# Four attention layers on one Trainium2 core: written orders for late fetches, additions and norms, and a quarter of a running sum moved to VectorE

## Chip, core and metric

The kernel runs on one core of a Trainium2 chip. The metric is the device time of one execution in microseconds; "before" is the median of three executions. The profile is one more execution, recorded by the hardware profiler. The engines are named as the profile names them: PE (TensorE, matmuls; PEld its weight loads), DVE (VectorE), ACT (ScalarE), POOL (GpSimd), SP (SyncE, which here only issues transfers).

## What is computed

Sixteen sequences of 56 tokens with 256 features pass through four layers. In each layer they attend to a memory of their own, 1500 rows of 128 features. Everything is float32. Cut to what matters, the reference is:

```python
def reference(x, ctx, mask, ...):                  # x 16x56x256, ctx 16x1500x128
    # L0: gated cross attention
    m = ctx @ W_mem
    c = softmax(x @ m.T / sqrt(D)) @ m
    x = rmsnorm(x + sigmoid(concat(x, c) @ W_gate + b) * c)
    # L1 (and L3, the same with other weights): masked cross attention, 16 heads, then a feed-forward part
    q = layernorm(x) @ Wq * scale;  k, v = split(ctx @ Wkv)
    x = x + tanh(attn_gate) * (softmax(where(mask, q @ k.T, lowest)) @ v) @ Wo
    x = x + tanh(ff_gate) * gelu(layernorm(x) @ W1) @ W2
    # L2: two experts (v, l) chosen by token, causal self attention, cross attention, MLP
    qkv = where(vm, rms(x) @ v_qkv, rms(x) @ l_qkv)
    x = x + where(vm, ctx_self @ v_dense, ctx_self @ l_dense)
    ck, cv = split(ctx @ ckv_w)                    # 16 heads of 8
    x = x + softmax(rms(x) @ cq_w @ ck.T) @ cv @ cdense_w
    mi = rms(x)
    x = x + where(vm, silu(mi @ v_gate) * (mi @ v_up) @ v_down,
                      silu(mi @ l_gate) * (mi @ l_up) @ l_down)
    # L3: as L1
    return x
```

The memory mask hides at most the last 375 of the 1500 rows.

## The kernel before

**Groups and items.** The 16 sequences ("batches") are four groups of four; a group has 224 tokens, kept as two tiles of 112 rows by 256. The pairs (layer, group) are sixteen items, k = 0 to 15. While an item's attention runs, side work is woven into it: the part behind the item before (`post`), and the part ahead of the next (`pre`). Side work is written as generators; `pace` and `step` draw pieces from them between the pieces of the attention, by shares that are written out by hand (`SHARES` for layer 2). The order in which the program emits the instructions is only a proposal: a scheduler puts them in the final order of each engine from the dependencies and its own estimates. Two copies of the program exist for two kinds of masks; the profiled execution runs the copy that masks the last 384 columns only.

**Layer 2's cross attention (`att2`).** Each batch has 12 chunks of 125 memory rows, taken as six pairs, one pair a step. All heads of a batch are 896 columns (4 row groups of PE, 224 columns each). One step of batch b, pair j, is:

- `weights_pair`: four banks of PSUM get the shifts (L1411, a matmul with ones) and then the scores (L1420, 32 matmuls in all); ScalarE takes the exponentials, one of 125x448 for each bank (L1425; 448 columns are both chunks of 224); then the weights are added into the running sum `all`, 125x896, in halves of 448 columns (L1437): POOL for batches 0 to 14, VectorE for batch 15. In the first pair of a batch there are two such additions, in each of the others four.
- `largest`: scores of the *next* batch for its maxima, four matmuls into four banks (L1374), and four reductions on VectorE (L1379). The maxima become the shifts (`shifts`, L1387 to L1400).
- `sums_chunk` (L1450): PE multiplies the weights of the pair before with the values.
- keys and values of coming batches (L1345, L1357), and pieces of side work.

Seven banks of PSUM rotate among all of these in the order of allocation; so the banks of the next L1411 come free only when the reductions L1379 of earlier banks are done. At the end of a batch `own_sums` (L1476 to L1484) takes the sums of `all` over its 125 rows with a matmul, and at the end of a group `close_group` (L1494) adds the result to the stream and starts the norm that is sorted by expert (`begin_norm`, sort: POOL scatters the rows to `sorted_rows`).

**Late side work in layer 2 (`late`, `beside`).** The part of L1 behind the attention (`post13`) runs for groups 2 and 3 only during layer 2; it has a `pause` between its two halves, and the second half begins with a layer norm: statistics on VectorE (L327, L328, L332), the root on POOL (L319), the normalization (L336, one operation for each of two tiles) on VectorE, and the turn by PE (L310 in `to_T`). Then `post2` takes the MLP of two groups at once: rows come from `sorted_rows` (`rows_of`), are turned (`to_T`, L310), multiplied (L1610), gated (L1617), multiplied back (L1629) and written to `made_rows`. `fetch` brings a group's rows back with two indirect transfers, issued by POOL (L1647); `take` adds them to the stream on VectorE (L1655) and begins the norm of L3. Groups 0 and 1 are taken while layer 2 still runs its group 3, groups 2 and 3 beside L3.

**L3's (and L1's) attention** takes rows of scores: L596 on PE, L599 on VectorE (mask and minimum), L603 on ScalarE (exponential), L633 the transposes, L614 the sums.

Of the kernel before, what the change touches and what calls it, by code (L numbers as in the profile page):

```python
# [15 lines left out]
AF = mybir.ActivationFunctionType  # L16
ALU = mybir.AluOpType
# [45 lines left out]
def tile_kernel(ctx: ExitStack, tc: tile.TileContext, a, layers=4, groups=NG):  # L63
# [239 lines left out]

    def to_T(xn, some=range(NT)):

        p = mm()
        w = len(some) * TP
        for c in range(2):
            for n, i in enumerate(some):
                nc.tensor.transpose(  # L310
                    p[:, c * w + n * TP : c * w + (n + 1) * TP],
                    xn[:, i, c * 128 : (c + 1) * 128],
                    ident[:TP, :TP],
                )
        return p[:, : 2 * w].rearrange("p (c t) -> p c t", c=2)

    def inverse_root(y, v):

        nc.gpsimd.tensor_tensor(y, v, half_less[:TP, : y.shape[-1]], ALU.pow)  # L319

    def begin_layernorm(g, gi, some=range(NT), engine=nc.gpsimd):
# [12 lines left out]
        xn = xpool.tile([TP, NT, D], F32, tag="xn", bufs=3, name="xn")  # L334
        for i in some:
            engine.tensor_scalar(  # L336
                xn[:, i, :], x[:, i, :], mv[:, 2 * i : 2 * i + 1], rstd[:, i : i + 1],
                ALU.subtract, ALU.mult,
            )
        begun[g, gi] = xn  # L340

    def layernorm_T(gi, g, b, some=range(NT)):
        if (g, gi) not in begun:
            begin_layernorm(g, gi, some, nc.vector)
            yield
            yield
        p = to_T(begun.pop((g, gi)), some)
        xT = xpool.tile([128, 2, T], F32, tag="xT", bufs=5, name="xT")[:, :, : len(some) * TP]
        gc, bc = VEC[g], VEC[b]
        for c in range(2):  # L350
            nc.vector.tensor_scalar(
                xT[:, c, :], p[:, c, :], vecs[:, gc + c : gc + c + 1],
                vecs[:, bc + c : bc + c + 1], ALU.mult, ALU.add,
            )
        return xT
# [224 lines left out]
    def rows(u):  # L580
# [12 lines left out]
        for i in range(RB):  # L593
            if u:
                sc = mm()
                nc.tensor.matmul(  # L596
                    sc[:, :LW], u["q"][:, i * 128 : (i + 1) * 128], u["kt"], start=True, stop=True
                )
                nc.vector.tensor_tensor_reduce(  # L599
                    u["p"][:, i], sc[:, :LW], u["mask"], 1.0, -LOWEST,  # L600
                    ALU.add, ALU.min, mn[:, i : i + 1],
                )
                nc.scalar.activation(  # L603
# [442 lines left out]
    def post13(name, gi, state, some=range(NT), pause=None):  # L1046
# [34 lines left out]
        w1, w2 = state["w1"], state["w2"]  # L1081
        xT = yield from layernorm_T(gi, name + "_ln_ff_g", name + "_ln_ff_b", some)
        yield
# [239 lines left out]
    PAIRS = NC // 2  # L1323
    SHARES = (2.1, 1.8), (2.1, 1.4), (2.1, 1.5), (1.8, 1.8)

# [39 lines left out]
    def largest(b, n):  # L1365
# [12 lines left out]
        for g in range(4):  # L1378
            nc.vector.tensor_reduce(  # L1379
                made["mx"][:, half * 4 + g, s : s + 1], banks[g][: 2 * N, :SW], AX.X, ALU.max  # L1380
            )

# [20 lines left out]
    def weights_pair(b, j):  # L1403
# [25 lines left out]
        if j == 0:  # L1429
            made["all"] = big.tile([128, 2, H, N], F32, tag="ot", name="all")[:CP, 0].rearrange(  # L1430
                "p h n -> p (h n)"
            )
        for c in range(0 if j else 1, 2):
            for lo in range(0, R, R // 2):
                cols = slice(lo, lo + R // 2)
                engine = nc.gpsimd if b + 1 < B else nc.vector
                engine.tensor_tensor(  # L1437
                    made["all"][:, cols], made["all"][:, cols] if j else p[:, 0, cols],
                    p[:, c, cols], ALU.add,
                )  # L1440

# [79 lines left out]
    def att2(gi, state, then, ends):  # L1521

        for k in range(G):
            b = gi * G + k
            for j in range(PAIRS):
# [15 lines left out]
                if ahead < B and not full:  # L1541
                    largest(ahead, n_ahead)
                if j + 2 == PAIRS and b + 1 < B:
                    shifts(b + 1)
# [24 lines left out]
    def post2(pair):  # L1569
# [21 lines left out]
        rows = rows_of(0)  # L1591
        yield
        yield
        for n, e in enumerate("vbl"):
            p = to_T(rows)
            xT = xpool.tile([128, 2, T], F32, tag="xT", bufs=5, name="xT")
# [46 lines left out]
    def fetch(gi):  # L1643

        y = tmp("back")[:TP]
        for i in range(NT):
            nc.gpsimd.indirect_dma_start(  # L1647
                y[:, i * D : (i + 1) * D], None, made_rows[gi // 2],
                bass.IndirectOffsetOnAxis(place_of(gi, i), 0),
            )  # L1650
        return y

    def take(gi, y):
        xf = xs[gi].rearrange("p i d -> p (i d)")
        nc.vector.tensor_add(xf, xf, y)  # L1655
        if gi < 3:
            begin_layernorm("L3_ln_q_g", gi)

    def program():
        line.update(turn=None, sum=None, side=iter(()), rate=1, closed=0, pair=None, due=0.0, share=0.0, k=0, behind=0, end=False, stage=0, beside=0)  # L1660
        for kept in (memory_w, halves_of, queries, heads_w, cross, held, begun):
# [23 lines left out]
        def beside(k):  # L1685
# [27 lines left out]
            if k == 3 * groups + 1:  # L1713
# [3 lines left out]
                yield  # L1717
                y = fetch(2)
                yield
                yield  # L1720
# [45 lines left out]
        def late():  # L1766
# [20 lines left out]
            y = fetch(0)  # L1787
            yield
            yield
            take(0, y)  # L1790
            line["stage"] += 1
            y = fetch(1)
            yield
            yield
            take(1, y)
# [211 lines left out]
```

## Time and profile before

| what | value |
|---|---|
| median of 3 runs | 1467.6 us (1466.56 to 1472.07) |
| the profiled execution's own time | 1461.5 us |
| its span | 1459.5 us |
| mean clock granted to PE | 0.981 of full speed |
| PE busy | 1370.9 us |
| 440–620 us: PE, DVE, ACT, POOL busy of 180 | 170.4, 97.3, 82.2, 108.8 |
| 620–780: of 160 | 152.3, 93.2, 78.5, 111.1 |
| 780–862: of 82 | 78.6, 54.4, 37.8, 56.1 |
| 862–1037: of 175 | 175.0, 90.5, 84.5, 140.8 |
| 1037–1060: of 23, clock 0.78 | 15.1, 9.0, 6.7, 17.7 |

The span goes from the first to the last instruction; some 2 us of the execution's time lie round it. Layer 2's cross attention runs from about 440 to 1085 us: group 0 to 620, group 1 to 780, group 2 to 862, and group 3 and the ends behind it. "Busy" sums the instructions of an engine in a stretch; the clock is what the throttle granted PE, where 1.0 is full speed. A wait is written "engine, tile, line <- the engine, tile and line that ended it", with its total, its count and the longest, in microseconds.

### The profile page before, as it was taken

The numbers are of one execution on the slowest core, as the hardware profiler recorded it, in microseconds if no ns is written. First come the engines' busy times: TensorE is split into PE (matmuls) and PEld (weight loads), VectorE is DVE, ScalarE is ACT, GpSimd is POOL, SyncE is SP. The second block draws the span as 40 slices with busy tenths as digits, with TensorE's granted clock in tenths as the row PEclk, the third lists the DMA queues.
The fourth block names the chain that finished last, engine by engine and source line by source line (L and its number), as shares of the span: only waits on it lengthen the run. The fifth ranks groups of instructions, "written<-read, shape, count | busy, mean of one in ns | idle before, by whom it ended". The sixth has DMA issues, their size and how long they took to land. (4 is left out here: it accounts for less than half of the span.)

```text
span 1459.5 us, 32402 instructions
## 1 busy us (share of the span) xinstructions
PE 1370.9 (94%) x13638; PEld 944.3 (65%) x13638; DVE 784.0 (54%) x1796; ACT 745.2 (51%) x1697; POOL 525.2 (36%) x567
## 2 busy tenths in 40 slices
PE   7989999999899989999999999999798999999997
PEld 4767777776655546555555556656466776777776
DVE  5344764557474753566546754554464345554641
ACT  2335767675533545444544544444365464756661
POOL 0021010100204656766577768787733111100000
PEclk9999999999999999999999999999899999999998
DMA  8943232331312011200110022131123343333320
GB/s 286 361 167 129 65 129 102 116 115 51 114 62 80 16 66 52 79 29 23 65 65 23 29 70 68 50 102 55 45 79 104 114 155 107 109 104 133 96 97 10
DMA packets 38808, 135.78 MB, mean 93 GB/s; under 512 B 8605, under 2 KB 18493, under 8 KB 34557
## 3 DMA queue, kind: packets, MB, share of 16 engines
q1 hardware_dynamic: 33901, 119.03, 23.8%
q0 software_dynamic: 2592, 10.85, 2.2%
q10 hardware_dynamic: 2160, 3.74, 0.7%
q8 instruction: 109, 1.79, 0.5%
q14 instruction: 46, 0.38, 0.1%
HBM read 129.01 MB, written 4.59 MB: 92 GB/s over the span
## 5 line engine op out<-in xcount | busy, mean ns | idle before, releaser
L1437 POOL TENSOR_TENSOR all<-all,pw 125x448 f32<-125x448 f32 x300 | 340.9, 1148 | 137.0 <-ACT pw L1425 126.7
L1379 DVE TENSOR_REDUCE mx<-sc 112x1 f32<-112x500 f32 x384 | 233.7, 669 | 127.7 <-PE sc L1374 127.5
L1425 ACT ACTIVATE pw<-sc 125x448 f32<-125x448 f32 x384 | 177.7, 550 | 116.2 <-PE sc L1420 113.2
L603 ACT ACTIVATE p<-p,few 128x384 f32<-128x384 f32 x224 | 136.9, 612 | 101.4 <-DVE few L599 100.7
L596 PE MATMUL sc<-ktl,qa 128*128 128x384 f32 x448 | 179.8, 510 | 0.0
L599 DVE CUSTOM_DVE_ANT_0 p<-sc,mkl 128x384 f32<-128x384 f32 x224 | 121.7, 551 | 93.7 <-PE sc L596 88.2
L614 PE MATMUL sc<-p,kvl 32*128 32x224 f32 x2160 | 153.7, 355 | 5.9 <-DVE qa L912 3.7
L614 PEld LDWEIGHTS sc<-p,kvl 32*128 32x128 f32 x2160 | 138.1, 186 | 22.3 <-issue 10.5
L614 PE MATMUL o<-p,kvl 32*128 32x224 f32 x720 | 146.8, 355 | 0.7 <-issue 0.6
L143 POOL TENSOR_SCALAR mkl<-m32l 128x384 bf16<-128x384 uint8 x32 | 16.3, 510 | 345.9 <-DVE few L599 300.2
L614 PEld LDWEIGHTS o<-p,kvl 32*128 32x128 f32 x720 | 131.5, 186 | 1.5 <-issue 1.5
L1374 PE MATMUL sc<-ck,qs 32*112 32x500 f32 x768 | 124.6, 625 | 4.1 <-DVE mx L1379 1.8
L302 ACT ACTIVATE p<-p,few 128x384 f32<-128x384 f32 x224 | 120.7, 609 | 7.5 <-DVE few L590 7.5
L633 DVE STREAM_TRANSPOSE p<-p 128x768 f32<-128x768 f32 (+1 forms) x96 | 103.0, 1095 | 23.0 <-ACT p L302 22.7
L596 PEld LDWEIGHTS sc<-ktl,qa 128*128 128x128 f32 x448 | 79.6, 193 | 37.5 <-issue 10.1
L1420 PE MATMUL sc<-qs,ck 32*125 32x224 f32 x1536 | 102.1, 362 | 0.0
L302 ACT ACTIVATE ot<-sc 128x224 f32<-128x224 f32 x64 | 32.0, 608 | 125.4 <-PE o L614 77.6
L1450 PE MATMUL o<-pw,vc 125*32 125x224 f32 x1536 | 95.8, 368 | 0.0
L1450 PEld LDWEIGHTS o<-pw,vc 125*32 125x32 f32 x1536 | 40.9, 111 | 70.1 <-issue 57.8
L319 POOL TENSOR_TENSOR stat<-stat,half_less 112x2 f32<-112x2 f32 (+1 forms) x33 | 23.1, 700 | 174.9 <-DVE stat L332 136.7
L1420 PEld LDWEIGHTS sc<-qs,ck 32*125 32x125 f32 x1536 | 79.6, 188 | 1.3
L1411 PE MATMUL sc<-shift,ones_r 2*125 2x448 f32 x384 | 61.5, 473 | 17.9 <-DVE mx L1379 15.4
(283 smaller groups left out, 2333.4 us busy)
## 6 DMA issues: line engine op xcount, KB each, us to landing
kvl<-in_ctx_last SPq DMA_DIRECT2D x30, 768.0 KB, 4.3
kt<-in_ctxT SPq DMA_DIRECT2D x23, 750.0 KB, 4.7
w<-in_L_W SPq DMA_DIRECT2D x16, 1024.0 KB, 4.8
w<-in_L_Wq SPq DMA_DIRECT2D x8, 1024.0 KB, 5.2
w<-in_L_Wo SPq DMA_DIRECT2D x8, 1024.0 KB, 4.8
ktl<-in_ctxT SPq DMA_DIRECT2D x32, 192.0 KB, 2.6
w<-in_L_v_qkv SPq DMA_DIRECT2D x4, 768.0 KB, 5.5
w<-in_L_l_qkv SPq DMA_DIRECT2D x4, 768.0 KB, 4.3
```

The costliest lines, as they stand in the source:

```text
L302: nc.scalar.activation(out, in_, AF.Copy, scale=scale)
L596: nc.tensor.matmul(sc[:, :LW], u["q"][:, i * 128 : (i + 1) * 128], u["kt"], start=True, stop=True)
L599: nc.vector.tensor_tensor_reduce(u["p"][:, i], sc[:, :LW], u["mask"], 1.0, -LOWEST, ALU.add, ALU.min, mn[:, i : i + 1],)
L603: nc.scalar.activation(u["p"][:, i], u["p"][:, i], AF.Exp, bias=mn[:, i : i + 1], scale=-1.0, accum_out=den[:, i : i + 1],)
L614: product = nc.tensor.matmul(o[g][:, : RB * BW], y["kv"][part, j, :], y["p"][part, :, j * BW : (j + 1) * BW], start=j == 0, stop=j == LB - ...
L633: nc.vector.transpose(blocks, blocks)
L1374: nc.tensor.matmul(banks[g][: 2 * N, :SW], made["q"][part, rows], made["k"][part, cols], start=True, stop=True,)
L1379: nc.vector.tensor_reduce(made["mx"][:, half * 4 + g, s : s + 1], banks[g][: 2 * N, :SW], AX.X, ALU.max)
L1420: nc.tensor.matmul(banks[g][:CP, c * QH : (c + 1) * QH], made["k"][part, at : at + CP], made["q"][part], start=False, stop=c == 1, skip_gr ...
L1425: nc.scalar.activation(p[:, :, g * QH : (g + 1) * QH], banks[g][:CP, : 2 * QH].rearrange("p (c n) -> p c n", c=2), AF.Exp,)
L1437: engine.tensor_tensor(made["all"][:, cols], made["all"][:, cols] if j else p[:, 0, cols], p[:, c, cols], ALU.add,)
L1450: nc.tensor.matmul(made["o"][part, :QH], made["v"][:, n, part], p[:, r * QH : (r + 1) * QH], start=n == 0, stop=n + 1 == NC, skip_group_ch ...
```

## The change

It has six parts. (1) A helper, `behind`, adds an ordering without a semaphore between two instructions: the first is put behind the second in the order that the scheduler makes. (2) The rows of pair 1 in `post2`: one more yield ahead of the first turn, and its transposes stand behind the last L596 that was emitted by then. (3) `begin_layernorm` gets a form for ScalarE: VectorE negates the mean (one small operation), and ScalarE subtracts it and multiplies with the root, two operations for each tile in place of VectorE's one. The late `post13` (groups 2 and 3) uses it. (4) `fetch` of groups 0 and 1 stands behind the last addition of weights on POOL, and `take`'s addition behind the last reduction of maxima (L1379) or of rows (L599). Four yields, not two, lie between fetch and take of groups 0 and 1, three, not two, for group 2. (5) The shares of groups 2 and 3 in layer 2 go from (2.1, 1.5) and (1.8, 1.8) to (2.1, 1.7) and (1.9, 1.9). (6) For batches 0 to 14 POOL adds the first three quarters of the weights' columns, in two operations of 336 columns where it had two of 448 for each chunk. VectorE adds the last 224 columns, which the fourth exponential makes; these additions are emitted at the end of the step's core, after the reductions of maxima. Batch 15 stays with VectorE in halves of 448.

```diff
--- before.py
+++ after.py
@@ -301,22 +301,34 @@
     def scalar_copy(out, in_, scale=1.0):
         nc.scalar.activation(out, in_, AF.Copy, scale=scale)
 
-    def to_T(xn, some=range(NT)):
+    def to_T(xn, some=range(NT), name=None):
 
         p = mm()
         w = len(some) * TP
         for c in range(2):
             for n, i in enumerate(some):
-                nc.tensor.transpose(
+                turned = nc.tensor.transpose(
                     p[:, c * w + n * TP : c * w + (n + 1) * TP],
                     xn[:, i, c * 128 : (c + 1) * 128],
                     ident[:TP, :TP],
                 )
+                behind(turned, name, "rows come late")
         return p[:, : 2 * w].rearrange("p (c t) -> p c t", c=2)
 
     def inverse_root(y, v):
 
         nc.gpsimd.tensor_tensor(y, v, half_less[:TP, : y.shape[-1]], ALU.pow)
+
+    def behind(made, name, reason):
+
+        if name:
+            tc.add_manual_dep(
+                made.ins, name,
+                mybir.DependencyInfo(
+                    mybir.DependencyClass.NoSync, mybir.DependencyReason.DATA
+                ),
+                reason=reason,
+            )
 
     def begin_layernorm(g, gi, some=range(NT), engine=nc.gpsimd):
 
@@ -332,16 +344,25 @@
         nc.vector.tensor_scalar(rstd[:, those], var, 1e-5, None, ALU.add)
         inverse_root(rstd[:, those], rstd[:, those])
         xn = xpool.tile([TP, NT, D], F32, tag="xn", bufs=3, name="xn")
-        for i in some:
+        if engine is nc.scalar:
+            less = stat(NT)[:TP]
+            mean = mv.rearrange("p (i s) -> p i s", s=2)[:, :, 0]
+            nc.vector.tensor_scalar(less, mean, -1.0, None, ALU.mult)
+            for i in some:
+                nc.scalar.activation(
+                    xn[:, i, :], x[:, i, :], AF.Identity, bias=less[:, i : i + 1]
+                )
+                scalar_copy(xn[:, i, :], xn[:, i, :], rstd[:, i : i + 1])
+        for i in () if engine is nc.scalar else some:
             engine.tensor_scalar(
                 xn[:, i, :], x[:, i, :], mv[:, 2 * i : 2 * i + 1], rstd[:, i : i + 1],
                 ALU.subtract, ALU.mult,
             )
         begun[g, gi] = xn
 
-    def layernorm_T(gi, g, b, some=range(NT)):
+    def layernorm_T(gi, g, b, some=range(NT), engine=None):
         if (g, gi) not in begun:
-            begin_layernorm(g, gi, some, nc.vector)
+            begin_layernorm(g, gi, some, engine or nc.vector)
             yield
             yield
         p = to_T(begun.pop((g, gi)), some)
@@ -593,13 +614,13 @@
         for i in range(RB):
             if u:
                 sc = mm()
-                nc.tensor.matmul(
+                line["scored"] = nc.tensor.matmul(
                     sc[:, :LW], u["q"][:, i * 128 : (i + 1) * 128], u["kt"], start=True, stop=True
-                )
-                nc.vector.tensor_tensor_reduce(
+                ).ins.name
+                line["drained"] = nc.vector.tensor_tensor_reduce(
                     u["p"][:, i], sc[:, :LW], u["mask"], 1.0, -LOWEST,
                     ALU.add, ALU.min, mn[:, i : i + 1],
-                )
+                ).ins.name
                 nc.scalar.activation(
                     u["p"][:, i], u["p"][:, i], AF.Exp, bias=mn[:, i : i + 1], scale=-1.0,
                     accum_out=den[:, i : i + 1],
@@ -1079,7 +1100,9 @@
         if "w2" not in state:
             (state["w2"],) = load_w((a[name + "_W2"], 8, D))
         w1, w2 = state["w1"], state["w2"]
-        xT = yield from layernorm_T(gi, name + "_ln_ff_g", name + "_ln_ff_b", some)
+        xT = yield from layernorm_T(
+            gi, name + "_ln_ff_g", name + "_ln_ff_b", some, nc.scalar if pause else None
+        )
         yield
         hT = big.tile([128, 8, T], F32, tag="hT", bufs=2, name="hT")[:, :, :w]
         per = 2 * T // w
@@ -1321,7 +1344,7 @@
 
     QH = 4 * N
     PAIRS = NC // 2
-    SHARES = (2.1, 1.8), (2.1, 1.4), (2.1, 1.5), (1.8, 1.8)
+    SHARES = (2.1, 1.8), (2.1, 1.4), (2.1, 1.7), (1.9, 1.9)
 
     def spread_queries(b):
 
@@ -1376,9 +1399,9 @@
                 start=True, stop=True,
             )
         for g in range(4):
-            nc.vector.tensor_reduce(
+            line["drained"] = nc.vector.tensor_reduce(
                 made["mx"][:, half * 4 + g, s : s + 1], banks[g][: 2 * N, :SW], AX.X, ALU.max
-            )
+            ).ins.name
 
     def shifts(b):
 
@@ -1430,14 +1453,21 @@
             made["all"] = big.tile([128, 2, H, N], F32, tag="ot", name="all")[:CP, 0].rearrange(
                 "p h n -> p (h n)"
             )
+        few_columns = 3 * R // 8 if b + 1 < B else R // 2
+        for lo in (0, few_columns):
+            add_weights(b, j, slice(lo, lo + few_columns), nc.gpsimd if b + 1 < B else nc.vector)
+
+    def add_weights(b, j, cols, engine):
+
+        made = cross[b]
+        p = made["p", j]
         for c in range(0 if j else 1, 2):
-            for lo in range(0, R, R // 2):
-                cols = slice(lo, lo + R // 2)
-                engine = nc.gpsimd if b + 1 < B else nc.vector
-                engine.tensor_tensor(
-                    made["all"][:, cols], made["all"][:, cols] if j else p[:, 0, cols],
-                    p[:, c, cols], ALU.add,
-                )
+            added = engine.tensor_tensor(
+                made["all"][:, cols], made["all"][:, cols] if j else p[:, 0, cols],
+                p[:, c, cols], ALU.add,
+            )
+            if engine is nc.gpsimd:
+                line["added"] = added.ins.name
 
     def sums_chunk(b, n):
 
@@ -1540,6 +1570,8 @@
                     sums_chunk(last, n + 1)
                 if ahead < B and not full:
                     largest(ahead, n_ahead)
+                if b + 1 < B:
+                    add_weights(b, j, slice(3 * R // 4, R), nc.vector)
                 if j + 2 == PAIRS and b + 1 < B:
                     shifts(b + 1)
                 if j == 1 and b:
@@ -1589,10 +1621,10 @@
         wc = VEC["L2_ln_post_attn_w"]
         wg, wu = (weights("v", w, 2, I2) for w in ("gate", "up"))
         rows = rows_of(0)
-        yield
-        yield
+        for _ in range(3 if pair else 2):
+            yield
         for n, e in enumerate("vbl"):
-            p = to_T(rows)
+            p = to_T(rows, name=line["scored"] if pair and not n else None)
             xT = xpool.tile([128, 2, T], F32, tag="xT", bufs=5, name="xT")
             for c in range(2):
                 nc.vector.tensor_scalar(
@@ -1644,20 +1676,22 @@
 
         y = tmp("back")[:TP]
         for i in range(NT):
-            nc.gpsimd.indirect_dma_start(
+            fetched = nc.gpsimd.indirect_dma_start(
                 y[:, i * D : (i + 1) * D], None, made_rows[gi // 2],
                 bass.IndirectOffsetOnAxis(place_of(gi, i), 0),
             )
+            if gi < 2:
+                behind(fetched, line["added"], "weights are added first")
         return y
 
     def take(gi, y):
         xf = xs[gi].rearrange("p i d -> p (i d)")
-        nc.vector.tensor_add(xf, xf, y)
+        behind(nc.vector.tensor_add(xf, xf, y), line["drained"], "banks go first")
         if gi < 3:
             begin_layernorm("L3_ln_q_g", gi)
 
     def program():
-        line.update(turn=None, sum=None, side=iter(()), rate=1, closed=0, pair=None, due=0.0, share=0.0, k=0, behind=0, end=False, stage=0, beside=0)
+        line.update(turn=None, sum=None, side=iter(()), rate=1, closed=0, pair=None, due=0.0, share=0.0, k=0, behind=0, end=False, stage=0, beside=0, added=None, drained=None, scored=None)
         for kept in (memory_w, halves_of, queries, heads_w, cross, held, begun):
             kept.clear()
         load_first()
@@ -1716,6 +1750,7 @@
                 yield
                 yield
                 y = fetch(2)
+                yield
                 yield
                 yield
                 take(2, y)
@@ -1785,13 +1820,13 @@
             yield
             yield
             y = fetch(0)
-            yield
-            yield
+            for _ in range(4):
+                yield
             take(0, y)
             line["stage"] += 1
             y = fetch(1)
-            yield
-            yield
+            for _ in range(4):
+                yield
             take(1, y)
             line["stage"] += 1
             while line["closed"] < 3 * groups:
```

## The prediction, made before the changed kernel ran

> **What bounds the kernel now.** I read the page's busy shares first, then the groups, the waits, and the timeline round each long wait. TensorE (PE) is busy 94% of the span; VectorE (DVE) 54%.
>
> ```profile
> PE 1370.9 (94%) x13638; PEld 944.3 (65%) x13638; DVE 784.0 (54%) x1796; ACT 745.2 (51%) x1697; POOL 525.2 (36%) x567
> ...
> L1437 POOL TENSOR_TENSOR all<-all,pw 125x448 f32<-125x448 f32 x300 | 340.9, 1148 | 137.0 <-ACT pw L1425 126.7
> L1379 DVE TENSOR_REDUCE mx<-sc 112x1 f32<-112x500 f32 x384 | 233.7, 669 | 127.7 <-PE sc L1374 127.5
> ```
>
> So 88.6 us of the 1459.5 are open to an edit that only orders work. The waits of PE name the pieces that this change aims at:
>
> ```profile
> PE sc L1411 <- DVE mx L1379: 15.4, 6, 7.9
> ...
> PE sc L310 <- DVE xn L336: 5.7, 2, 3.2
> ...
> PE sc L310 <- DMA rows<-sorted: 5.3, 2, 3.9
> ```
>
> Each line gives total, count and longest. The longest maxima wait is seen whole in the timeline: VectorE sits 5.86 us in take(0)'s addition, waiting for a fetch, while finished score banks lie undrained behind it.
>
> ```profile
> 1043.46 0.69 DVE L1655 TENSOR_TENSOR x<-x,back 112x512 f32<-112x512 f32 x1 [5.86 <-DMA back<-made,place]
> ...
> 1047.89 2.43 DVE L1379 TENSOR_REDUCE mx<-sc 112x1 f32<-112x500 f32 x4
> ...
> 1048.62 0.73 PE L1411 MATMUL sc<-shift,ones_r 2*125 2x448 f32 x1 [7.88 <-DVE mx L1379]
> ```
>
> Then the clock is low: 1045.0 to 1055.2 is granted half speed, and 16 scores take 2.22 us where they took 0.93 at 943.5. PE idles until 1048.6 anyway, so 6.6 us of half clock lose 3.3. The same pattern, shorter, stands at 530.58 (2.72 us, then 6.8 us at half clock) and 703.15 (2.74 us, then 3.4):
>
> ```profile
> 530.25 2.41 DVE L336 TENSOR_SCALAR xn<-x,stat 112x256 f32<-112x256 f32 x2 [3.14 <-POOL stat L319]
> ...
> 532.58 1.25 DVE L1379 TENSOR_REDUCE mx<-sc 112x1 f32<-112x500 f32 x2
> ```
>
> VectorE waits 3.14 us for POOL's root (late post13's norm), with maxima behind it.
>
> **The change, part by part.** *Fetch and take(0).* The addition moves behind the last maxima, (14,3). All 11.2 us (7.88 + 3.3) would go, but in the built order L3's turns (L310 of group 0) now stand directly after L1394, ahead of L1411 of step (14,5). They need, after the maxima: the addition 0.69, L327/L328/L332 1.9, POOL's root 0.72, two POOL L336 of 1.22: 5.8 us; PE has 2.5 us of work queued ahead of them. New stall 3.3, with 1.7 of half clock likely: gain 6.2, say **6**; bounds 0 (the new wait as long as the old) and 11. The four fetch instructions (0.93 each) move past POOL's additions and are split in two; POOL is idle 20% there (140.8 busy of 175 us), which covers them; without it they would put 1.9 us per pair on the additions.
>
> *Late norms.* For groups 2 and 3 DVE's two L336 (0.62 each) become four ScalarE operations per group, plus one DVE negation of 0.17. Nothing of VectorE waits for POOL's root there any more. ScalarE waits instead; behind it are the Exps, but ScalarE is busy 82 of 180 us in 440–620, and four operations at L302's 0.61 make 2.4 per group. The stalls with their half clock are 2.72 + 3.3 and 2.74 + 1.7 = 10.5. An Exp held behind that ScalarE wait, up to 3.14, gives part back: **7**, bounds 3 and 10.
>
> [...]
>
> *Rows' turns of pair 1.* One more L596 pair (0.81) goes ahead of the transposes, into the 3.92 us wait for rows<-sorted: 0.8 for certain, 2.5 if 3.4 us of half clock behind it goes too (1.7): **1.5** (0.7 to 2.5).
>
> *take(2), fetch(2) and L3's norms.* One yield more and an addition behind L599: gaps of 1.4 and up to 3.3 of half clock may go, but the norm begins some 6 us later against PE's order, with 2 more L596 (0.8) as cover: 0 (-3 to +4). L3's ff norm at 1238.7 gets L901 ahead of it against 3.18 us: +1 (-1 to +2.5). Shares only repace side work, seen in the order above: nothing extra. Sum of gains 15.5, some **15** (7 to 25).
>
> *A quarter of the columns.* POOL's 330 additions shrink from 448 to 336 columns, 1.133 to 0.85 us, 93 us of POOL. Nobody waits for that: the view of L1437 shows 0.9 for L1476 and 0.7 for L1425. VectorE gets 165 additions of 125x224, two in a step (one in a pair's first). In the built order they stand *ahead of* the maxima in nearly every step from the second on, and they wait for the fourth Exp. Behind them are four maxima, behind those the banks of the next L1411. Their price:
>
> ```profile
> L1437 POOL TENSOR_TENSOR all<-all,pw x300: 1118/1133/1522, 457.3 to 1066.5; 125x448 f32<-125x448 f32 x150
> L1437 DVE TENSOR_TENSOR all<-all,pw x20: 617/624/626, 1068.7 to 1085.1; 125x448 f32<-125x448 f32 x20
> L1437 DVE TENSOR_TENSOR all<-pw x2: 1555/1589/1623, 1062.3 to 1063.9; 125x448 f32<-125x448 f32 x2
> ```
>
> The same VectorE addition takes 0.624 us alone and 1.589 while POOL adds (until 1067.6): 0.965 more, 85% of one POOL addition. With 224 columns: alone 0.39 (L1617, 128x224, has 0.385), beside POOL 0.39 + 0.85 x 0.85 = 1.1. Bounds of a pair are 0.78 and 2.2; POOL is busy 60 to 80% of these stretches and works just after the same Exps, so I take 2.05.
>
> [...]
>
> What a pair costs depends on the step. In tight steps (604–608) last Exp to maxima to L1411 close a loop:
>
> ```profile
> 604.83 1.85 ACT L1425 ACTIVATE pw<-sc 125x448 f32<-125x448 f32 x4 [0.75 <-PE sc L1420]
> ...
> 606.88 2.44 DVE L1379 TENSOR_REDUCE mx<-sc 112x1 f32<-112x500 f32 x4 [2.06 <-PE sc L1374]
> ```
>
> From one L1411 block to the next is 4.46 us. With additions between: Exps 2.5, pair 2.05, two maxima 1.3, L1411 0.1: 5.95, 1.5 more in some 10 steps = 15. In the 27 steps of 862–1037, where PE is 100% busy at 6.05 a step, a gated product (0.4) joins: 6.4, at most 0.3 each, 8; PE's queued side work covers part: 6. Where self attention leaves VectorE 4.4 to 7.1 us busy of 6.1 to 7.2, 2.05 more overflow by some 3 us in each of three groups: 9. Sum **30**. Bounds: an uncontended pair (0.78) costs 0.3 in the tight steps, 3, and 2 elsewhere: 5; everything contended, without cover, 52.
>
> Net 30 - 15.5 = +14.5 on the profiled run's 1461.5 (span 1459.5 and 2.0 round it): 1476. That run lies 6.1 below the median of the runs, 1467.6; I put the difference on the median: **1482**.
>
> **Rivals.** *Cheap additions (faster).* If POOL and VectorE rarely meet, VectorE's additions cost 5 and the orders' 15.5 win: -10.5, **1457**, down to 1446 with gains of 25 against 3. For it: POOL's additions are 36% of the span, and reductions from banks show 0.669 beside POOL, undisturbed. Against it: both engines start from the same Exp. It decides as soon as a pair stays under about 1.3 us. *Repeated half clock (slower).* Gaps of 1.40 to 2.74 were followed by half clock; if ten of the tight steps' new 1.5 us gaps do it too, 3.4 us each at half speed, 17 more: **1499**. Against it: the 1.5 us gaps at 496.3, 668 and 832 were not. *Moved stalls.* The change does not do what it says: take(0)'s norm wait replaces its fetch wait (gain 0 instead of 6), ScalarE's wait the one of VectorE (3 instead of 7), and additions are cheap (5 of 0 + 3 + 1.5 + 1 = 5.5): **1467**, no change.
>
> **How the numbers follow.** Contended additions 0.45 (own range 1467 to 1500: additions of 18 to 45 against gains of 18 to 12.5); cheap ones 0.33; repeated half clock 0.13; moved stalls 0.09. About 0.5% (7.3 us) is what a measurement here tells from no change. Slower: 0.39 of the first and 0.13: 0.52. Faster: 0.29 of the second and 0.03 of the fourth: 0.32. Same: the rests, 0.06 of the first, 0.04 of the second, 0.06 of the fourth: 0.16. The range reaches to both rivals' ends, 1446 and 1505.
>
> **What would show it.** Right: L1437's VectorE group near 1.0 us mean, more waits of PE's L1411 on L1379 than 15.4, 862–1037 no longer at 175 busy; the 7.88, 2.72 and 2.74 stalls gone; a 3 us wait of L310 near 1043. Wrong: a mean near 0.4 to 0.5 there, with PE's busy time higher than 94%. The forecast falls too if the scheduler's queued PE work covers the longer loop.

## The result, and the profile after

The changed kernel takes 1522.5 us where the one before takes 1469.2: a ratio of 1.038 (95% interval 1.035 to 1.041), 53 us slower. That is the side that was forecast and far outside the range (1446 to 1505). The profiled run has a span of 1520.7 us. Its line numbers are those of the changed kernel: L1411 of before is L1434 (shifts), L1420 is L1443 (scores), L1425 is L1448 (exponentials), L1437 is L1465 (additions), L1374 is L1397 and L1379 is L1402 (maxima).

The page after, the same parts as shown of before, busy time first, then groups:

```profile
PE 1419.4 (93%) x13638; PEld 968.4 (64%) x13638; DVE 863.8 (57%) x1959; ACT 748.3 (49%) x1705; POOL 467.6 (31%) x567
...
L1465 POOL TENSOR_TENSOR all<-all,pw 125x336 f32<-125x336 f32 x300 | 283.6, 955 | 210.1 <-ACT pw L1448 199.3
...
L1402 DVE TENSOR_REDUCE mx<-sc 112x1 f32<-112x500 f32 x384 | 233.6, 664 | 17.1 <-PE sc L1397 17.0
L1465 DVE TENSOR_TENSOR all<-all,pw 125x224 f32<-125x224 f32 (+1 forms) x170 | 112.2, 663 | 167.1 <-ACT pw L1448 164.6
```

The maxima are as short as before (0.664 us, 0.669 before), but the wait ahead of them has changed hands: VectorE waited 127.5 us for their banks before, and 17.0 now. In place of that it waits for the exponentials, with the maxima queued behind. The view of the waits says the same (total, count, longest), and that PE's weight loads pay for it. Before:

```profile
PEld sc L1411 <- DVE mx L1379: 28.1, 32, 8.2
```

The longest of these, 8.2 us, is the stall at take(0) that the prediction shows; without it 19.9 us remain. After:

```profile
DVE all L1465 <- ACT pw L1448: 189.7, 82, 6.9
...
PEld sc L1434 <- DVE mx L1402: 40.0, 79, 2.5
...
DVE mx L1402 <- PE sc L1397: 17.0, 14, 2.8
```

One step in the timeline (start, length, engine, line):

```profile
806.86 1.85 ACT L1448 ACTIVATE pw<-sc 125x448 f32<-125x448 f32 x4 [2.47 <-PE sc L1443]
807.92 3.95 POOL L1465 TENSOR_TENSOR all<-all,pw 125x336 f32<-125x336 f32 x4 [2.04 <-ACT pw L1448]
...
808.75 1.39 DVE L1465 TENSOR_TENSOR all<-all,pw 125x224 f32<-125x224 f32 x2 [2.25 <-ACT pw L1448]
810.14 2.43 DVE L1402 TENSOR_REDUCE mx<-sc 112x1 f32<-112x500 f32 x4
811.07 0.84 PE L1434 MATMUL sc<-shift,ones_r 2*125 2x448 f32 x4
```

The chain is the one that the prediction drew: last exponential (808.71), pair of additions, maxima, shifts. The pair takes 1.39 us beside POOL's additions: 0.39 for the first and 0.97 for the second, medians over the 66 pairs. The first one mostly starts when a POOL addition is nearly over (in 60 pairs one is under way, with 0.07 us left in the median), the second when another has just begun (in 52, 0.28 us ago).

From the first shifts of a group's first batch to those of the next group's, the timeline gives 170.4 us before and 182.0 after for group 0, 164.1 and 185.7 for group 1, 161.5 and 180.8 for group 2, 116.8 and 120.7 for group 3 up to batch 15. Groups 0 to 2 lose 52.5 us; group 3, beside which the matmuls of `post2` run, loses 3.9. (In the profile before, the steps of group 2 run to 943 us, not to 862 as said ahead of the prediction: 862–1037 holds the second half of group 2 and most of group 3.) And the clock has fallen there. The windows view of 440 to 900 us (busy time of PE, PEld, DVE, ACT, POOL, then the granted clock, DMA share, GB/s), before:

```profile
440.00:900.00 460.00, 439.22 (x4953) 260.03 (x4954) 265.44 (x501) 217.78 (x460) 307.31 (x308) 0.99 0.14 50
```

and after:

```profile
440.00:900.00 460.00, 431.30 (x4546) 250.69 (x4544) 291.17 (x559) 197.83 (x415) 233.06 (x271) 0.94 0.13 44
```

In both profiles the clock granted is either full or half; of these 460 us, 10.2 were at half clock before and 51.3 after. Half of the difference, 20.6 us, is the most of PE's work that half clock can have cost there: as far as PE had work. The profiled run before began with 7 us less in its first 90 us, where the two programs hold the same work, so 61 us lie between the two spans and 53 between the medians.

### The profile page after: what moved, and what is told of

Its sections match the earlier page's. It is cut to its first block, busy times and chain, and to the rows that moved or that the text cites. A ratio compares the mean times of both kernels' runs of the same rounds, so it can differ in the third digit from the quotient of the medians.

```text
span 1520.7 us, 32612 instructions
## 1 busy us (share of the span) xinstructions
PE 1419.4 (93%) x13638; PEld 968.4 (64%) x13638; DVE 863.8 (57%) x1959; ACT 748.3 (49%) x1705; POOL 467.6 (31%) x567
## 5 line engine op out<-in xcount | busy, mean ns | idle before, releaser
L1465 POOL TENSOR_TENSOR all<-all,pw 125x336 f32<-125x336 f32 x300 | 283.6, 955 | 210.1 <-ACT pw L1448 199.3
L1448 ACT ACTIVATE pw<-sc 125x448 f32<-125x448 f32 x384 | 177.7, 549 | 137.3 <-PE sc L1443 122.8
L1402 DVE TENSOR_REDUCE mx<-sc 112x1 f32<-112x500 f32 x384 | 233.6, 664 | 17.1 <-PE sc L1397 17.0
L1465 DVE TENSOR_TENSOR all<-all,pw 125x224 f32<-125x224 f32 (+1 forms) x170 | 112.2, 663 | 167.1 <-ACT pw L1448 164.6
L1397 PE MATMUL sc<-ck,qs 32*112 32x500 f32 x768 | 126.3, 639 | 4.8 <-DVE mx L1402 2.1
L1443 PE MATMUL sc<-qs,ck 32*125 32x224 f32 x1536 | 111.3, 377 | 0.0
L1434 PE MATMUL sc<-shift,ones_r 2*125 2x448 f32 x384 | 86.2, 487 | 17.5 <-DVE mx L1402 10.6
L1434 PEld LDWEIGHTS sc<-shift,ones_r 2*125 2x125 f32 x384 | 35.4, 186 | 81.6 <-DVE mx L1402 40.0
```

The lines of the kernel that those rows point to most:

```text
L1397: nc.tensor.matmul(banks[g][: 2 * N, :SW], made["q"][part, rows], made["k"][part, cols], start=True, stop=True,)
L1402: line["drained"] = nc.vector.tensor_reduce(made["mx"][:, half * 4 + g, s : s + 1], banks[g][: 2 * N, :SW], AX.X, ALU.max).ins.name
L1434: nc.tensor.matmul(banks[g][:CP, : 2 * QH].rearrange("p (c n) -> p c n", c=2), ones_r[rows], made["shift"][rows].unsqueeze(1).to_broadcast ...
L1443: nc.tensor.matmul(banks[g][:CP, c * QH : (c + 1) * QH], made["k"][part, at : at + CP], made["q"][part], start=False, stop=c == 1, skip_gr ...
L1448: nc.scalar.activation(p[:, :, g * QH : (g + 1) * QH], banks[g][:CP, : 2 * QH].rearrange("p (c n) -> p c n", c=2), AF.Exp,)
L1465: added = engine.tensor_tensor(made["all"][:, cols], made["all"][:, cols] if j else p[:, 0, cols], p[:, c, cols], ALU.add,)
```

## The experiments

**The two halves of the change.** First the change without VectorE's quarter, and the quarter alone on the kernel before:

```diff
-        few_columns = 3 * R // 8 if b + 1 < B else R // 2
+        few_columns = R // 2
...
-                if b + 1 < B:
-                    add_weights(b, j, slice(3 * R // 4, R), nc.vector)
```

> The changed kernel without VectorE's quarter: POOL adds all columns in halves of 448 again, the other five parts stay. Theory Q (VectorE's additions are the whole loss, the orders gain what was forecast): about 1454 us, 15 below the 1469 of before. Rival O (the written orders themselves lose, the additions only part): above 1480 us. Rival N (the stalls only moved, the orders are worth nothing): 1465 to 1472 us.

> The kernel before with VectorE's quarter alone. Theory Q: the additions cost what the orders gain more than the whole change lost, 53 + 15, so about 1535 us. Rival O: under 1500 us. Rival N: about 1522 us, the same as the whole change.

Orders alone: 1467.5 us, ratio 1.0003 (0.998 to 1.002). Quarter alone: 1521.5, ratio 1.038 (1.036 to 1.040). So rival N holds: the quarter is the whole loss, and five parts that were forecast to gain 15 us together gain nothing.

**Why the quarter costs 54: its place.** The same additions behind the maxima of their step, or one step later in the program:

```diff
             if engine is nc.gpsimd:
                 line["added"] = added.ins.name
+            elif b + 1 < B:
+                behind(added, line["drained"], "maxima first")
```

> The changed kernel, with each of VectorE's quarter additions placed by a written order behind the reductions of maxima that were emitted before it. Same work, same engines, only the place in VectorE's queue. Theory W (the loss is the wait: maxima whose banks are full stand behind an addition that waits for the fourth exponential): most of the loss comes back, 1460 to 1480 us, with VectorE's waits for L1402's banks up again from 17 us. Rival T (the loss is VectorE's added time and the contention with POOL, wherever it stands): 1510 us or more.

```diff
-                if b + 1 < B:
-                    add_weights(b, j, slice(3 * R // 4, R), nc.vector)
+                late_b, late_j = (b, j - 1) if j else (b - 1, PAIRS - 1)
+                if 0 <= late_b < B - 1:
+                    add_weights(late_b, late_j, slice(3 * R // 4, R), nc.vector)
```

> The changed kernel, with VectorE's quarter of a pair added one step later, at the same place in its queue: the exponentials are then long done, so there is no wait left, while number, size and place of the additions stay. Theory W: most of the loss comes back, 1460 to 1485 us, with the pair's time still added ahead of the maxima. Rival T: 1510 us or more.

Behind the maxima: 1472.5, ratio 1.003 (1.0005 to 1.0053). Of 55 us, 50 are gone with number, size and engine unchanged; VectorE's wait for the banks is back at 108.9 us. (The additions also take less time there: 85.3 us in sum for 106.7, 0.53 for 0.67 in the mean of the 150 behind the first pairs.) The second run (1524.7) looks like theory T and tells nothing: the scheduler, which orders by its own estimate of readiness, put the later-written additions where they had been. VectorE's list of instructions is the same as the changed kernel's, apart from line numbers.

**Wait or length.** An addition of 8 columns in the same place, and one that becomes ready with the first exponential, not the fourth:

```diff
-        few_columns = 3 * R // 8 if b + 1 < B else R // 2
+        few_columns = (R - 8) // 2 if b + 1 < B else R // 2
...
-                    add_weights(b, j, slice(3 * R // 4, R), nc.vector)
+                    add_weights(b, j, slice(R - 8, R), nc.vector)
```

> The changed kernel, but VectorE adds only the last 8 of the 896 columns and POOL two times 444: each of VectorE's additions stays at its place in the queue and waits for the fourth exponential, and takes about 0.1 us, not 0.39 to 1.0. Theory W (the wait for the exponential ahead of finished maxima is the loss): 1495 us or more. Rival L (the loss is the length of the additions in the loop from exponential to maxima to the next shifts): 1470 to 1480 us. In between, the two share the loss in that proportion.

```diff
         for lo in (0, few_columns):
+            lo += R // 4 if b + 1 < B else 0
...
-                    add_weights(b, j, slice(3 * R // 4, R), nc.vector)
+                    add_weights(b, j, slice(0, R // 4), nc.vector)
```

> The changed kernel, but VectorE adds the first 224 columns, which the first exponential of the pair makes, and POOL the last three quarters: the same work, the same place in the queue, but the additions are ready some 1.4 us earlier (three exponentials of 0.46). Theory W: the wait ahead of the maxima shortens by 1.4 us in the steps where it ends last: 1475 to 1500 us. Rival C (length beside POOL decides): 1510 us or more.

Narrow: 1499.4, 32 us above before, though each addition is short (0.17 us where it starts just ahead of a POOL addition, 0.32 where one is under way): more than half of the loss stays when the length is nearly gone. That is not the wait alone, since POOL's additions still run beside it; see below. First quarter: 1477.5, 45 us less than the changed kernel, for additions that are ready 1.4 us earlier. Their view of L1465 (here L1466) shows why 1.4 us do so much: the pair runs ahead of POOL's additions, which now start with the last exponentials, and not beside them; its sum falls from 106.7 to 84.1 us. One step of its timeline:

```profile
808.58 1.85 ACT L1448 ACTIVATE pw<-sc 125x448 f32<-125x448 f32 x4 [0.71 <-PE sc L1443]
809.15 0.82 DVE L1466 TENSOR_TENSOR all<-all,pw 125x224 f32<-125x224 f32 x2 [1.16 <-ACT pw L1448]
810.07 2.73 POOL L1466 TENSOR_TENSOR all<-all,pw 125x336 f32<-125x336 f32 x3 [2.73 <-ACT pw L1448]
```

**Contention.** Two runs left out POOL's additions in pairs 1 to 5, with and without the quarter, and were spoilt by the way in which that was done: a constant had to be added in pair 0, by two more operations of POOL (1.33 us each without the quarter), ahead of the product that VectorE's reduction L1464 waits for, with maxima behind it.

> The changed kernel with POOL's additions left out in pairs 1 to 5 of a batch (the sums of three quarters of the columns are incomplete; a constant is added in the first pair so that they are not zero). VectorE's pair then runs without POOL beside it, near 0.8 us where it took 1.39. Theory W: the time stays at 1510 us or more. Rival C (contention with POOL lengthens the additions, and that is the loss): 1490 us or less, with VectorE's additions at 0.39 each.

> The written orders without VectorE's quarter, and with POOL's additions left out in pairs 1 to 5 of a batch (incomplete sums of all columns; a constant is added in the first pair). It is the base of the run in which POOL's additions were left out and VectorE's quarter stayed (1488.8). Theory WC (wait and contention share the loss): 1460 to 1467 us, so that the quarter without contention costs 22 to 29 and contention with POOL the rest of the 55. Rival W (the place in the queue is nearly all, POOL's absence merely makes other work faster): 1445 to 1455 us, so that the quarter costs 34 to 44 even without contention.

1488.8 and 1489.5: the first lies where rival C expected it, the second far above both of its expectations, and neither answers the question. The pair was run again with one POOL operation in place of the addition in pair 0, and none elsewhere:

```diff
+            if b + 1 == B or not j:
                 add_weights(b, j, slice(lo, lo + few_columns), ...)
...
+        if engine is nc.gpsimd:
+            line["added"] = engine.tensor_scalar(
+                made["all"][:, cols], p[:, 0, cols], 1.0, None, ALU.add
+            ).ins.name
+            return
```

> The written orders without VectorE's quarter; POOL touches the sums once a batch (in the first pair it writes weights plus one, in place of the addition; all other additions of POOL are left out, so the sums are incomplete). The base for the next one, without the longer work of POOL in the first pair that the two earlier runs without additions had. Theory P (that longer work, ahead of the product that VectorE's L1464 of before waits for, was what made them slow): 1455 to 1468 us. Rival: 1480 us or more again.

> The changed kernel with POOL's additions left out in the same way: VectorE's quarter as changed, each addition 0.39 us, no POOL beside it. Against the last one it gives the price of the place in the queue with the pair's bare 0.8 us. Theory WC (wait and contention share the loss of 55): 20 to 35 us above the last one. Rival W (all is the wait): 45 us or more above it. Rival C (all is contention): under 10 us above it.

| medians, us | without the quarter | with the quarter in its place |
|---|---|---|
| POOL touches the sums once a batch | 1457.4 | 1476.8 |
| POOL adds as in the changed kernel | 1467.5 | 1522.5 |

Without POOL beside it the quarter costs 19.4: the wait, and a pair of 0.8 us. (The eleven runs with the quarter spread from 1471 to 1485, so this is good to a few us.) With POOL it costs 55.0: 35.6 us come only from both together. VectorE's wait for the exponentials ahead of these additions is the same in all three kernels: 189.7 us in the changed one, 191.7 with 8 columns, 191.4 without POOL's additions. What differs is the length of the additions, 0.39 each without POOL's, 0.39 and 0.97 with them, and the clock. The windows view of 440 to 900 us with the quarter and without POOL's additions:

```profile
440.00:900.00 460.00, 439.47 (x4872) 259.01 (x4867) 284.60 (x606) 217.20 (x461) 62.92 (x92) 0.99 0.14 49
```

The clock is 0.99 there and 0.94 in the changed kernel; over whole executions it is 0.972 to 0.980 in all runs of the one and 0.958 to 0.962 in all runs of the other. So POOL's additions beside the quarter lengthen the pair by 0.6 us, and half clock takes up to 23 of the 35.6 us (0.05 of 460). That the longer pair is what lowers the clock is not shown, and the kernel with 8 columns speaks against it. Its pair takes 0.5 us, less than the 0.8 without POOL, and yet its clock is lower and it loses more (32 us):

```profile
440.00:900.00 460.00, 434.44 (x4749) 254.22 (x4747) 277.13 (x586) 207.29 (x436) 284.06 (x285) 0.96 0.14 47
```

With POOL's additions and no quarter the clock is 0.99 too (the orders alone); why it is lower when both engines add stays open.

**Why the orders gain nothing.** Late norms by ScalarE alone, then fetch and take of groups 0 and 1 alone, both on the kernel before, with the edits as in the diff:

> The kernel before with the changed kernel's late norms alone: groups 2 and 3 normalized by ScalarE. Theory S (the wait for POOL's root only changes its engine: behind ScalarE's second operation stand the step's exponentials, and the stall of PE stays near 2.5 us): 1464 to 1468 us, within 3 us of before. Rival G (the forecast's gain of 7): 1460 us or less.

> The kernel before with the changed kernel's fetches and additions of groups 0 and 1 alone. Theory S (the stall of 7.9 is cut into pieces: the shifts' chain L1387 to L1390 behind take's addition, then L3's turns behind POOL's norm): 1464 to 1470 us. Rival G (the forecast's gain of 6): 1461 us or less.

The norms: 1466.2, ratio 0.998 (0.996 to 1.0005): at most a small gain. Fetch and take: 1476.3, ratio 1.006 (1.003 to 1.008): slower by 8. Where the norms' gain went is seen in the run of the orders alone, which has the same stall on another engine:

```profile
530.70 0.91 ACT L302 ACTIVATE xn<-xn,stat 112x256 f32<-112x256 f32 x2 [2.14 <-POOL stat L320]
531.51 1.82 ACT L1448 ACTIVATE pw<-sc 125x448 f32<-125x448 f32 x4
...
532.09 1.09 PE L1397 MATMUL sc<-ck,qs 32*112 32x500 f32 x2 [2.50 <-ACT pw L1448]
```

ScalarE's second operation waits for POOL's root, the exponentials stand behind it, their banks stay full, and PE stalls 2.50 us where it stalled 2.72. POOL computes this root late since it first finishes another norm (L393, 1.83 us).

Fetch and take alone still stall 6.9 us, and then 10.3 (that kernel's numbers: L1670 is L1655 of before, L1401 and L1405 are L1390 and L1394, L890 is L879):

```profile
1053.05 0.69 DVE L1670 TENSOR_TENSOR x<-x,back 112x512 f32<-112x512 f32 x1 [5.63 <-DMA back<-made,place]
...
1054.73 0.97 PE L1405 MATMUL sc<-ident,minus 112*32 112x112 f32 x16 [6.89 <-DVE minus L1401]
...
1071.95 0.69 DVE L1670 TENSOR_TENSOR x<-x,back 112x512 f32<-112x512 f32 x1 [15.76 <-DMA back<-made,place]
...
1074.19 2.24 PE L890 MATMUL sc<-xT,w 128*128 128x224 f32 x5 [10.34 <-DVE xT L362]
```

The addition is behind the last maxima, as ordered, but ahead of the chain from maxima to shifts. And the second fetch, now held behind later additions of POOL, lands so late that its addition holds up a norm's copy for PE. With the new shares beside it:

```diff
-    SHARES = (2.1, 1.8), (2.1, 1.4), (2.1, 1.5), (1.8, 1.8)
+    SHARES = (2.1, 1.8), (2.1, 1.4), (2.1, 1.7), (1.9, 1.9)
```

> The kernel before with the fetches and additions of groups 0 and 1 as changed, and the two new pairs of shares for layer 2. Theory H (the shares bring post2 of groups 0 and 1 to its end earlier, and so the fetched rows; without them the same orders cost 8): 1465 to 1470 us. Rival X (the shares do nothing, the other parts of the change make up for the 8): 1474 to 1479 us.

1467.0, ratio 1.001 (0.9996 to 1.003): theory H holds. The shares end `post2` earlier (its last rows of groups 0 and 1 are sent off 5 us earlier, counted from the first shifts), and the stalls shrink to 2.9 (shifts' chain), 2.6 and 0.8 (L310), in sum near the 7.9 of before.

> The written orders without VectorE's quarter and without what the change does to group 2 (the third yield between its fetch and take, and the place of its addition behind L599). Theory T2 (the 4.5 us stall of L310 in L3 at 1209 is made by that part): 1461 to 1465 us, under the 1467.5 of all orders. Rival N: 1466 to 1470 us.

1466.8: the part at group 2 makes no difference in time (rival N). The stall of 4.5 at L310 falls to 1.1, and one of 3.2 takes its place (L1113, L3's feed-forward matmuls).

**Attempts at better orders.** Each took the wait from one queue and found it in the next.

> The kernel before with one edit: the two late norms (groups 2 and 3 of L1) are normalized by POOL, which also computes their root, where VectorE did it before and ScalarE does in the changed kernel. Theory M (any engine whose queue holds work of the step passes the wait on; POOL computes the root itself and nothing waits soon for what is behind it): the stalls of 2.7 us at 530 and 703 go, 1458 to 1464 us. Rival N (the wait comes back as a stall of PE at the turn L310): 1465 to 1470 us.

> The last one, and the fetches and additions of groups 0 and 1 in a written order again, with two differences from the changed kernel: take's addition stands behind the copy of the shifts (L1400 of before), not only behind the maxima, and two more yields follow it before L3's turns may start. Theory M: 6 to 11 us less than the last one, 1450 to 1456 us, no stall of PE above 3 us between 1035 and 1060. Rival N: within 3 us of the last one.

> The kernel before with one order changed on VectorE: each late norm's two L336 stand behind the four maxima that they stood ahead of; nothing else moves on any engine. Theory P (only the place in the queue counts; POOL's root is ready by the time that the maxima are done, and the turns that need the norm come later): the stalls of 2.7 at 530 and 703 go, with up to 5 us of half clock: 1457 to 1463 us. Rival S (the wait moves to PE's turns L310 of the norm): 1465 to 1470 us.

> The kernel before with other orders for groups 0 and 1: the four fetches of both groups are issued together behind the last additions of their step, take's addition stands behind the copy of the shifts L1400, and L3's turns of group 0 stand two blocks of shifts later on PE. Theory P: the stall of 7.9 at 1040 goes and none above 2 us takes its place before 1085: 1457 to 1462 us. Rival S: 1465 us or more, with a new wait that the trace names.

Norms by POOL: 1472.0, ratio 1.003 (1.002 to 1.005). The two 2.7 us gaps became 0.9 at L310 and 3.04 at the shifts: POOL's product of L1463 comes later, the reduction that needs it waits 5.81 us, and the maxima behind it wait too (that kernel's L1466, L1381 and L1413 are L1464, L1379 and L1411 of before):

```profile
550.40 0.53 DVE L1466 TENSOR_REDUCE rest<-rest 128x56 f32<-128x224 f32 x1 [5.81 <-POOL rest L1463]
550.85 2.42 DVE L1381 TENSOR_REDUCE mx<-sc 112x1 f32<-112x500 f32 x4
551.57 0.28 PEld L1413 LDWEIGHTS sc<-shift,ones_r 2*125 2x125 f32 x1 [3.25 <-DVE mx L1381]
```

With the mended fetches on top: 1478.1, ratio 1.0075 (1.0055 to 1.0095), with a stall of 4.7 at L310 and one of 5.9 at L3's first matmuls. Norm behind the maxima on VectorE: 1466.3, ratio 0.999 (0.998 to 1.001); 2.7 became 1.0 and 0.8 at L310. Both fetches first: 1478.7, ratio 1.008 (1.005 to 1.011); the 7.9 became 7.1 at L310, since the rows land after the last step that could cover the norm. No version that computes everything beats the kernel before by more than the noise.

## Why the prediction was wrong

**Bound, place and chain: right.** PE's loop through exponential, additions, maxima and shifts was named, the additions were placed ahead of the maxima, and behind them the banks; moving them behind the maxima gives 50 of 55 us back.

**The price of a pair: too high, and still the sum was too low.** 2.05 us were taken; 1.39 were measured, since the first of the two additions, with 0.39 in the median, seldom waits long for POOL. The second takes 0.97, which is 0.58 more, beside POOL additions of 0.90. Only 4 of 66 pairs took more than the 2.2 us of the prediction's upper bound.

**The step that failed: the steps with self attention, and half clock left out of the sum.** The sum of 30 for the additions had "some 3 us in each of three groups" (9) for the steps with self attention, 15 for some ten tight steps, 6 for the 27 steps of 862–1037, and nothing for half clock. The starts of the shifts in the traces give what each part lost, and the clock records how long half clock lasted; half of that time is the most that it can have cost. The first figure compares the changed kernel with the one of the orders alone, the second the kernel with the quarter alone with the one before:

| steps | forecast, us | lost, us | half clock in it, at most |
|---|---|---|---|
| first twelve of groups 0, 1 and 2 (self attention) | 9 | 30.6; 37.0 | 17.1; 20.5 |
| last twelve of groups 0 and 1 (here are the tight steps) | 15 | 13.9; 8.2 | 3.4; 1.7 |
| the next 27 (862–1037 before) | 6 | 9.5; 10.7 | 1.7; 1.7 |
| sum | 30 | 54.0; 55.9 | 22.2; 23.9 |

So the steps with self attention lost three to four times their 9 us; half clock can be a little over half of it. PE stands there for VectorE's work on the self attention, which the additions push back. Three such stalls, of up to 2.19 us, are new (L1368 is L1345 of before, keys; L1162 is L1139, self attention's scores less their maxima):

```profile
671.27 2.39 DVE L1465 TENSOR_TENSOR all<-all,pw 125x224 f32<-125x224 f32 x2 [1.54 <-ACT pw L1448]
...
673.59 1.14 DVE L1161 TENSOR_REDUCE stat<-sc 120x8 f32<-120x448 f32 x2
674.65 1.14 DVE L1162 TENSOR_TENSOR s<-sc,stat 120x448 f32<-120x448 f32 x2
...
675.41 1.21 PE L1368 MATMUL sc<-kt,l2w 128*128 128x500 f32 x2 [2.19 <-DVE s L1162]
```

Apart from half clock the three parts lost 32 us, near the 30 forecast. That is luck in part, for the pair was priced too high, and the part with self attention (13.5 to 16.6 without half clock) too low. Nor is the loss confined to ten steps: some 40 of the 72 steps of groups 0 to 2 are over 0.3 us longer. Before, VectorE waited for the scores (127.5 us) and its maxima freed their banks at once; now they stand behind additions that wait for the exponentials (189.7 us). The waits of PE's weight loads for maxima went from 32 (19.9 us without the stall at take(0)) to 79 (40.0 us).

**Half clock was a rival, and should have been a term.** That "the 1.5 us gaps at 496.3, 668 and 832 were not" followed by it was read from single gaps. In groups 0 to 2 of the changed kernel PE has 19 gaps of 0.5 to 2.2 us where it had 10 (1.1 to 2.7 us), and the clock is 0.94 over 460 us. The rival's 17 was nearly the size (22 to 24 at most, by the table); what was wrong is to set it beside the forecast as a case by itself, when the additions beside POOL's bring it about: without POOL's the clock stays at 0.99. That the gaps pull the clock down is not shown. With 8 columns PE has 15 such gaps and a clock of 0.96, without POOL's additions 13, none above 1.7 us, and 0.99.

**The orders: 15 forecast, 0 measured.** Norms by ScalarE: 7 forecast, 2.7 measured, not clear of zero; the sentence on "An Exp held behind that ScalarE wait" named what happened, and gave it 3.5 of 10.5 us where it takes most. Fetch and take: 6 forecast, -8 alone; the wait of L310 was seen, the chain L1387 to L1390 behind the addition was not, nor the second fetch. "Shares only repace side work" and "nothing extra" was wrong: they are worth 6 to 9 us to these fetches (1476.3 to 1467.0, ratios 1.006 to 1.001). The rival of moved stalls, given 0.09, is what the orders did. Rows' turns and the part at group 2: too small to tell.

The cheap-additions rival fell because of the wait: even at 0.39 us each, without POOL, they cost 19.4, not 5.

## What to carry to other kernels

Here additions that wait for an exponential, standing in VectorE's order ahead of the maxima that free PE's banks, cost 55 us; the same additions behind the maxima cost 5. So before work goes to an idle engine, ask what stands behind it and how much slack the loop has, and put it behind what others wait for. A stall that is moved to another queue is only gone if that queue holds nothing urgent behind it: PE's stall of 2.72 us behind VectorE's norm came back as 2.50 by way of ScalarE, and by way of POOL as 0.9 and 3.04. And look at the granted clock as well as at the waits: here it fell from 0.99 to 0.94 over 460 us and took up to 24 of 55 us, so a price for it belongs into the sum.

## What had not been expected of the hardware

Of VectorE's additions for batches 0 to 14 that started while a POOL addition of the weights ran, 137 of 138 in the changed kernel and all 85 in the kernel with 8 columns ended only after it. With 224 columns the first of a pair took 0.39 us, the second, begun some 0.28 us into a POOL addition, 0.97 (medians); with 8 columns it was 0.17 or 0.32. Without POOL's additions the whole is 10 us shorter (1457.4 against 1467.5), though hardly anything waits for them: in the run of the orders alone 1.6 us in two waits is the most that any one line's waits for L1465 come to. Layer 2's first shifts start between 446.7 and 456.0 us in the profiled runs of the twenty kernels, which hold the same work until then; nearly all of the difference arises in the first 90 us, with half-clock intervals in different places (3.4 us of them in the first 100 us of the profile before, 13.7 in that of the changed kernel). A part of the spread of the runs of the kernel before (1461 to 1479) may arise there too.
